# A list scheduler's estimated lengths are replaced by other ones, and its model of the port and of transposes is rewritten

## Chip, cores and metric

The kernel runs on one core of one Trainium2 chip. The metric is the device time of one execution in microseconds; the time of a kernel is the median of several executions. Before the change three executions gave 1193.82, 1195.94 and 1197.42 us.

## What is computed

A "macaron" block on x of shape 4 x 2048 x 256 in float32: half a feed-forward, one causal attention head, half a feed-forward, each behind a layernorm and with a residual. All feed-forward products run on operands that are first rounded, in blocks of 16, to a 4-bit grid.

```python
x = x + 0.5 * ffn(layernorm(x), w_gate, w_up, w_down)
x = x + attn(layernorm(x), Wq, Wk, Wv)          # causal softmax, scale 1/16
x = x + 0.5 * ffn(layernorm(x), w_gate, w_up, w_down)

def fp4_linear(x, w):                            # both sides rounded per block of 16
    return einsum('bsk,nk->bsn', fp4(x), fp4(w))
def fp4(x):
    scale = max(max(abs(block)) / 6, 1e-12)
    return nearest_on_grid(block / scale) * scale   # 0 .5 1 1.5 2 3 4 6, signed
def ffn(x, w_gate, w_up, w_down):                # 256 -> 704 -> 256
    return fp4_linear(silu(fp4_linear(x, w_gate)) * fp4_linear(x, w_up), w_down)
```

## The kernel before

**Tiling.** The 8192 rows are cut into 32 "pairs" of 2 x 128 rows (8 pairs for each of the 4 sequences). A pair n passes through these steps, each a small function of the kernel; the names are used below:

- `load(n)`, `ln_first(n)`: DMA of the rows (tile `xt`), first layernorm. Sums and squares are on ScalarE (ACT), a chain of seven two-element operations (`ve`, `rs`, `r2` ..., `nm`; tiles with prefix f, a or g for the three layernorms) on GpSimd (POOL), and the last scaling on ACT again (tile `xn`).
- `x1(n)`: the rounding of `xn` (tiles `xs`, `xinv`, `xf`, `xsh`, `xsl`) on VectorE (DVE) and ACT, and a DMA transpose to `xqT`.
- `gu1(n)`: 48 matmuls, for each half pair 12 into a gate tile `pg` and 12 into an up tile `pu`; ACT applies silu to `pg`, DVE multiplies with `pu` (tile `h`). `pg` and `pu` have one PSUM buffer each, so the next gate matmuls wait until ACT has read the last ones.
- `hh1(n)`: the rounding of `h` (tiles `hs`, `hinv`, `hf`, `hsh`, `hsl`) on DVE and ACT, two DMA transposes to `hT`.
- `down1(n)`: 2 x 17 matmuls on `hT` into `po`, and a DVE operation that adds them to `xt`.
- `lnattn(n)`, `xattn(n)`, `vy(n)`: second layernorm, two transposes to `xT`, the products for values (`vv`) and for the combined query/key matrix (`y`).
- `scores(n,j)`, `exps(n,j)`, `pv(n,j)` for each half pair j: scores into `ps`, copied out by DVE into `sc` with a running maximum (`mc`, `mr`, `nb`); exp on ACT; a split into two float16 halves (`pp`), one to three transposes to `pT`; the product with `vv` into `po`, scaled by `rc` and added to `xt`.
- `lnlast(n)`, `x2`, `gu2`, `hh2`, `down2(n)`: the third layernorm and the second feed-forward, and the store of the rows.

`prepare_gu`, `prepare_dn` and `prepare_attn` round, scale and transpose the weights at the start. The last pair (31) is finished in two half pairs, called z0 and z1 below; its steps are written out at the end of the kernel.

**Order.** All operations are first only recorded, in a software-pipelined order (pairs n+6 to n-3 in one step). Then `order` plans: a list scheduler (`_pass`) plays the five instruction queues PE, ACT, DVE, POOL and SP with an estimated length (`_cost`: time on the engine, `busy`, and time until a reader may use the result, `late`) for each operation, and emits them in the order of planned start. It is run forward and backward 6 times for each of 15 settings in `POLICIES` (how far ahead an operation may be taken, how strongly waiting counts, how far the first steps are pulled forward: `lead`), the setting that loses least planned PE time is kept for each half of the run, and one last pass writes the order. The order on each engine is then fixed: an instruction waits for its operands, and all that stands behind it in its queue waits too. All DMA is issued from SP's queue. Each instruction is emitted from one line (`emit`, line 362 of the profile), so groups are told apart by their tiles.

**What the plan knows of POOL and the transposes.** POOL shares a port to the on-chip memory with DVE. Before, a POOL operation is not planned while a DVE operation that takes the port (`op.locks`) runs; it is put off, and DVE operations that lock get a malus of `PORT` meanwhile. Transposes are planned as one queue (`served`) with 1.7 ns an element.

Of the kernel before, what the change touches and what calls it, by code (L numbers as in the profile page):

```python
# [12 lines left out]
F32 = mybir.dt.float32  # L13
# [4 lines left out]
AF = mybir.ActivationFunctionType  # L18
ALU = mybir.AluOpType
# [33 lines left out]
LN2 = 0.6931471805599453  # L53
BYTES = {F32: 4, I32: 4, F16: 2, BF16: 2, U16: 2}
SWITCH = 17600.0
PORT = 500.0
ROUNDS = 6
POLICIES = [(soon, 60.0, lead) for lead in (0.0, 10000.0, 20000.0) for soon in (50.0, 100.0, 150.0, 200.0, 300.0)]
MIDDLE = 500000.0
RATE = 330.0  # L60
LATENCY = 1900.0
WINDOW = 3413.0
IDLE = 0.42

# [90 lines left out]
class Record:  # L155
# [53 lines left out]
    def _cost(self, op):  # L209

        size = lambda v: v.at.size
        views = op.outs + op.ins
        n = max(map(size, views[:1] + (op.ins[:1] if op.method == "tensor_reduce" else [])))
        psum = any(v.tile.pool.psum for v in views)
        accum = isinstance(op.kwargs.get("accum_out"), View)
        if op.engine == "PE":
            t = max(n, 64) / 2.4 + 2.2
            if op.ins[0].dtype == F32:
                t *= 2 if op.method == "transpose" or "is_transpose" in op.kwargs else 4
            return t, t + 65  # L220
        if op.engine == "SP":
            if op.method == "dma_start_transpose":
                return 1240, 2250 + max(0, n - 500) * 1.2
            op.load = n * 4 * P / RATE if op.outs else 0
            return 490, LATENCY + op.load + 500 * (not op.outs)
        if op.engine == "POOL":
            t = 110 if op.method == "memset" else 850 if ALU.pow in op.args else 350
            return t, t
        if op.engine == "ACT":
            t = 95 + n * (0.75 if psum else 0.833) + 90 * accum  # L230
            t += 90 * sum(isinstance(op.kwargs.get(k), View) for k in ("scale", "bias"))
            return t, t + 105 * (not accum)
        many = sum(size(v) > 1 for v in op.ins)
        op.locks = not psum and (many > 1 or op.method == "tensor_scalar" and BYTES[op.ins[0].dtype] == 2)
        fast = not psum and all(BYTES[v.dtype] == 2 for v in views)
        if op.method == "reciprocal":
            t = 60 + 6.25 * n
        else:
            t = 65 + n * (1.042 if not fast else 0.26 if op.method == "tensor_scalar" else 0.52) + 65 * accum
        return t, t + 95  # L240

    def order(self):

        for pool in self.pools:
            for ring in pool.rings.values():
                for k, t in enumerate(ring):
                    if k >= t.n:
                        t.first.deps.update(dict.fromkeys(ring[k - t.n].ops, True))  # L250
                    if k:
                        t.first.deps.setdefault(ring[k - 1].first, False)
                    t.first.deps.pop(t.first, None)
        for op in self.ops:
            for u in op.after:
                op.deps.setdefault(u, False)
            op.users = {}
        for op in self.ops:
            for u, data in op.deps.items():
                u.users[op] = u.late + 24 if data else u.busy  # L260

        best = [None, None]
        for policy in POLICIES:
            lead = {op: op.lead * policy[2] for op in self.ops}
            rank = {op: 88.0 * op.index - lead[op] for op in self.ops}
            for _ in range(ROUNDS):
                start, out, end = self._pass(rank, False, policy, policy)
                for h, value in enumerate(self._lost(start, end)):
                    if best[h] is None or value < best[h][0]:
                        best[h] = (value, policy, start, rank)  # L270

                back, _, _ = self._pass({op: -start[op] - op.busy for op in self.ops}, True, policy, policy)
                rank = {op: -back[op] - op.busy - lead[op] for op in self.ops}
        (_, one, start, rank1), (_, two, _, rank2) = best

        part = {op: min(1.0, max(0.0, (start[op] - MIDDLE) / 50000.0 + 0.5)) for op in self.ops}
        rank = {op: rank1[op] * (1.0 - part[op]) + rank2[op] * part[op] for op in self.ops}
        return self._pass(rank, False, one, two)[1]
# [7 lines left out]
    def _pass(self, rank, back, one, two):  # L286


        free = dict.fromkeys(("PE", "ACT", "DVE", "POOL", "SP"), 0.0)
        waiting, held = {e: [] for e in free}, ("PE", "POOL")  # L290
        ready, start = dict.fromkeys(self.ops, 0.0), {}
        if back:
            nxt, left = {op: [] for op in self.ops}, {op: len(op.users) for op in self.ops}
            for op in self.ops:
                for v, lag in op.users.items():
                    nxt[v].append((op, v.busy + lag - op.busy))
        else:
            nxt, left = {op: list(op.users.items()) for op in self.ops}, {op: len(op.deps) for op in self.ops}
        for op in self.ops:
            if not left[op]:  # L300
                waiting[op.engine].append(op)
        kept = False
        table, out, end, landed, served, locked, clock = None, [], 0.0, 0.0, 0.0, 0.0, Counter()
        while len(out) < len(self.ops):
            best = None
            if not any(waiting.values()):
                raise RuntimeError("the order goes in a circle")
            for e, ops in waiting.items():
                if ops:
                    t = max(free[e], min(ready[op] for op in ops))  # L310
                    if best is None or t < best[0]:
                        best = (t, e)
            t, e = best
            soon, patience = (one if t < MIDDLE else two)[:2]
            now = [op for op in waiting[e] if ready[op] <= t + soon]
            op = min(now, key=lambda o: (
                rank[o] + patience * max(0.0, ready[o] - t) + SWITCH * (o.table is not None and o.table != table)
                + PORT * (kept and e == "DVE" and o.locks)
            ))
            t = max(t, ready[op])  # L320
            if e == "POOL" and not back and op.method != "memset":

                kept = t < locked
                if kept:
                    free[e] = locked + 1.0
                    continue
            if op.table is not None and op.table != table:
                table, t = op.table, t + 1290
            waiting[e].remove(op)
            out.append(op)  # L330
            start[op], more = t, 0.0
            if back:
                pass
            elif e == "PE":

                k = int(t // WINDOW)
                more = op.busy if k and clock[k - 1] < IDLE * WINDOW else 0.0
                clock[k] += op.busy + more
            elif op.load:
                landed = max(landed, t + LATENCY) + op.load  # L340
                more = landed - t - op.late
            elif e == "SP" and op.outs:
                served = max(served + 1.7 * op.outs[0].at.size + 100, t + op.late)
                more = served - t - op.late
            elif e == "DVE" and op.locks:
                locked = t + op.busy
            elif e == "POOL" and op.method != "memset":
                more = (775.0 if ALU.pow in op.args else 275.0) - op.busy
            free[e] = t + op.busy + (more if e in held else 0.0)
            end = max(end, t + op.late + more)  # L350
            for u, lag in nxt[op]:

                ready[u] = max(ready[u], t + lag + (more if e in held or u.deps.get(op) else 0.0))
                left[u] -= 1
                if not left[u]:
                    waiting[u.engine].append(u)
        return start, out, end
# [787 lines left out]
```

## Time and profile before

| | before |
|---|---|
| median of three runs | 1195.94 us (1193.82 to 1197.42) |
| the profiled execution's own time | 1194.8 us |
| span of that execution on the core | 1193.1 us |
| PE busy | 1156.1 us, 97% |
| DVE busy | 1064.1 us, 89% |
| ACT busy (84 table loads of 1283 ns among it) | 845.4 us, 71% |
| POOL busy | 254.9 us, 21% |
| DMA transposes | 411 issues of four kinds, median 2.5 to 3.8 us to landing |

Busy times are those of the profiled execution; they are unions of the instructions' spans, and a matmul's end is modelled, so a busy PE may still lose a little between matmuls. The time outside the span is 1.7 us. Each text line of the profile's groups has engine, operation, result and operands by tile name, and how often.

### The profile page before, as it was taken

To read this page: it belongs to the slowest core of one execution; us is meant where nothing else is said; L and a number is where in the kernel's file an instruction comes from. 1 tells how busy PE (TensorE), PEld (TensorE's weight loads), DVE (VectorE), ACT (ScalarE), POOL (GpSimd) and SP (SyncE) were. 2 spreads that over 40 slices of the span, in tenths; PEclk is the share of its full clock that TensorE was granted. 3 is DMA by queue.
4 is the path that set the end of the run, shared out by engine and by line. 5 is a ranking of instruction groups with operands and counts; after the bars stand their busy time and mean duration, and the time that the engine had idled before them with its cause. 6 is when DMAs were issued, how large, how long until landed. Compare 5 with 4: busy or idle time off the path is not lost.

```text
span 1193.1 us, 23867 instructions
## 1 busy us (share of the span) xinstructions
PE 1156.1 (97%) x8665; PEld 843.8 (71%) x8665; DVE 1064.1 (89%) x2677; ACT 845.4 (71%) x1694; POOL 254.9 (21%) x706
## 2 busy tenths in 40 slices
PE   3999999999999999999999999999999999999997
PEld 1676677777687777777777777777777777777775
DVE  8998999998879999998888999999887999978776
ACT  8788886676568777775776986776758776766552
POOL 4122331121032222212222230222212222010020
PEclk9999999999999999999999999999999999999999
DMA  7353646763665565655755465666556454665553
GB/s 236 55 100 71 109 88 110 140 129 71 107 131 103 105 116 120 113 93 111 134 102 81 95 114 104 131 131 120 92 104 113 88 93 87 114 117 96 102 111 85
DMA packets 452710, 128.92 MB, mean 108 GB/s; under 512 B 434672, under 2 KB 451824, under 8 KB 452592
## 3 DMA queue, kind: packets, MB, share of 16 engines
q1 hardware_dynamic: 452592, 127.39, 57.0%
q8 instruction: 68, 1.11, 0.4%
q14 instruction: 50, 0.41, 0.1%
HBM read 11.34 MB, written 8.39 MB: 17 GB/s over the span
## 4 chain that ended last, share of the span: by engine, by line
PE 68%; DVE 15%; ACT 12%; issue 2%; DMA 2%; POOL 1%; SPq 0%; DVEq 0%; ACTq 0%
PE po L362 30%; PE pg L362 14%; PE pu L362 14%; PE ps L362 10%; DVE h L362 5%; ACT xn L362 3%; ACT L362 2%; DVE hs L362 2%; ACT hf L362 2%; ACT h L362 1%; DVE xt L362 1%; DMA hT<-h 1%; ACT pp L362 1%; DVE xs L362 1%; DVE sc L362 1%
## 5 line engine op out<-in xcount | busy, mean ns | idle before, releaser
L362 PEld LDWEIGHTS <-xqT 128*128 128x128 f16 x3072 | 299.7, 98 | 161.1 <-issue 6.2
L362 PE MATMUL po<-wdT,hT 128*128 128x256 f16 x2176 | 262.6, 274 | 5.9 <-DMA hT<-h 5.6
L362 PE MATMUL pg<-wguT,xqT 128*128 128x384 f16 (+1 forms) x1536 | 258.9, 312 | 4.3 <-ACT h L362 2.3
L362 PE MATMUL pu<-wguT,xqT 128*128 128x384 f16 (+1 forms) x1536 | 253.3, 312 | 0.1
L362 PEld LDWEIGHTS <-hT 128*128 128x128 f16 x2176 | 213.2, 98 | 39.8 <-DMA hT<-h 7.6
L362 PE MATMUL ps<-xT,y 128*128 128x512 f16 (+2 forms) x960 | 200.9, 347 | 1.0 <-DVE mc L362 1.0
L362 PE MATMUL po<-vv,pT 128*128 128x257 f16 (+1 forms) x1632 | 194.4, 272 | 0.4
L362 PEld LDWEIGHTS <-pT 128*128 128x128 f16 x1632 | 157.9, 97 | 33.3 <-issue 2.3
L362 ACT ACTIVATE h<-pg,cgu 128x704 f32<-128x704 f32 x128 | 108.1, 845 | 93.9 <-PE pg L362 91.2
L362 DVE TENSOR_TENSOR h<-h,pu 128x704 f32<-128x704 f32 x128 | 113.2, 884 | 50.9 <-PE pu L362 33.4
L362 PEld LDWEIGHTS <-y 128*128 128x128 f16 x960 | 90.9, 98 | 69.6 <-ACT y L362 1.2
L362 ACT ACTIVATE hf<-h 128x1408 f16<-128x1408 bf16 (+1 forms) x65 | 88.1, 1355 | 65.1 <-DVE h L362 65.0
L362 ACT ACTIVATE sc<-sc,nb,ksc 128x128 f32<-128x128 f32 (+7 forms) x64 | 82.7, 1292 | 38.6 <-DVE nb L362 38.0
L362 ACT ACT_TABLE_LOAD x84 | 107.8, 1283 | 2.1 <-PEq L1138 0.8
L362 DVE TENSOR_REDUCE hs<-h 128x88 f32<-128x1408 f32 (+1 forms) x65 | 103.7, 1595 | 1.0
L362 DVE TENSOR_TENSOR h<-h,hinv 128x1408 f32<-128x1408 f32 (+1 forms) x65 | 103.8, 1597 | 0.4
L362 DVE TENSOR_SCALAR_CACHE_REDUCE sc<-ps 128x512 f32<-128x512 f32 (+2 forms) x144 | 84.7, 595 | 11.5 <-PE ps L362 11.2
L362 DVE TENSOR_TENSOR pp<-sc,pp 128x1024 f16<-128x1024 f32 (+4 forms) x96 | 86.1, 907 | 5.7 <-ACT pp L362 5.0
L362 POOL TENSOR_SCALAR gve<-gsq 128x2 f32<-128x2 f32 (+1 forms) x33 | 9.4, 284 | 380.3 <-ACT xn L362 380.2
L362 POOL TENSOR_SCALAR ave<-asq 128x2 f32<-128x2 f32 x32 | 14.1, 439 | 327.4 <-ACT xn L362 277.7
L362 ACT CAST pp<-sc 128x1024 f16<-128x1024 f32 (+4 forms) x96 | 73.1, 789 | 1.0
L362 DVE SCALAR_TENSOR_TENSOR xt<-po,het,xt 128x256 f32<-128x256 f32 x128 | 59.5, 464 | 11.7 <-PE po L362 11.6
(153 smaller groups left out, 1593.6 us busy)
## 6 DMA issues: line engine op xcount, KB each, us to landing
xt<-x SPq DMA_DIRECT2D x32, 256.0 KB, 3.3
out<-xt SPq DMA_DIRECT2D x31, 256.0 KB, 2.6
pT<-pp SPq DMA_TRANSPOSE x152, 3.0
hT<-h SPq DMA_TRANSPOSE x128, 3.8
gu<-wgu SPq DMA_DIRECT2D x3, 384.0 KB, 5.0
xqT<-xn SPq DMA_TRANSPOSE x65, 3.2
xT<-xs SPq DMA_TRANSPOSE x64, 2.5
dwork<-wdn SPq DMA_DIRECT2D x1, 704.0 KB, 7.3
```

Source lines behind the costliest of these rows:

```text
L362: op.call(*map(real, op.args), **{k: real(v) for k, v in op.kwargs.items()})
```

## The change

Only the plan's model is edited; no operation of the computation is added, removed or altered. The lengths in `_cost` change (TensorE's results are taken as readable 176 ns instead of 65 ns after the matmul, POOL operations as 154 and 647 ns instead of 350 and 850, transposes as longer by their size, accumulating DVE operations as shorter, those with a per-row scalar as longer). The lag between an operation and its reader depends on the two engines (`_lag`). The malus `PORT` and the putting off of POOL operations are gone: a POOL operation that starts while DVE holds the port is planned as ending 35 ns before DVE does, and it is taken only when ready. A table load begins when ACT's queue is free. Instructions are themselves fetched by DMA; the plan now counts the instructions of PE, DVE and ACT, foresees when the next block is fetched (`FETCH`), and takes a transpose that meets such a fetch as late by 0.7 or 1.5 us; SP's queue is held when transposes back up.

```diff
-PORT = 500.0
+FETCH = {
+    "PE": (2.0, 256.0, 118.0, 64.0, 1500.0),
+    "DVE": (1.16, 128.0, 55.0, 470.0, 700.0),
+    "ACT": (1.26, 128.0, 60.0, 700.0, 700.0),
+}
...
-            return t, t + 65
+            return t, t + 176
...
-                return 1240, 2250 + max(0, n - 500) * 1.2
+                return 1280 + 0.13 * n + 0.75 * max(0, n - 1408), 1850 + 1.26 * n
...
-            return 490, LATENCY + op.load + 500 * (not op.outs)
+            return 570, LATENCY + op.load + 500 * (not op.outs)
...
-            t = 110 if op.method == "memset" else 850 if ALU.pow in op.args else 350
-            return t, t
+            t = 110 if op.method == "memset" else 647 if ALU.pow in op.args else 154
+            return t, t + 28
...
-            return t, t + 105 * (not accum)
+            t += 33 * (AF.Silu in op.args)
+            return t, t + 105
...
-            t = 65 + n * (1.042 if not fast else 0.26 if op.method == "tensor_scalar" else 0.52) + 65 * accum
+            t = 65 + n * (1.042 if not fast else 0.26 if op.method == "tensor_scalar" else 0.52) + 10 * accum
+            t += 62 * (op.method in ("tensor_scalar", "scalar_tensor_tensor") and any(size(v) == 1 for v in op.ins[1:]))
...
+    def _lag(self, u, op):
+        if op.engine == "POOL":
+            return 94 if u.engine == "POOL" else 101
+        return 81 if u.engine == "PE" and op.method == "tensor_tensor" else 48 if u.engine == "ACT" and op.engine == "PE" else 24
...
-                u.users[op] = u.late + 24 if data else u.busy
+                u.users[op] = u.late + self._lag(u, op) if data else u.busy
...
+            if e == "POOL":
+                soon = 0.0
...
-                + PORT * (kept and e == "DVE" and o.locks)
...
-            if e == "POOL" and not back and op.method != "memset":
-                kept = t < locked
-                if kept:
-                    free[e] = locked + 1.0
-                    continue
...
-                table, t = op.table, t + 1290
+                table, t = op.table, max(t, free[e] + 1400)
...
+            if e in FETCH:
+                i = list(FETCH).index(e)
+                per, block = FETCH[e][:2]
+                issued[i] += per - (e == "PE" and op.ins[0].dtype == F32)
+                if issued[i] > coming[i]:
+                    fetched[i], coming[i] = t, coming[i] + block
...
-                served = max(served + 1.7 * op.outs[0].at.size + 100, t + op.late)
-                more = served - t - op.late
+                begin = max(served, t + 1400)
+                served = begin + 1.26 * op.outs[0].at.size
+                held_up = 0.0
+                for i, (_, _, _, each, lost) in enumerate(FETCH.values()):
+                    for f in (fetched[i], t + max(0.0, coming[i] - issued[i]) * each):
+                        if begin - lost < f < served + 50:
+                            held_up = max(held_up, lost - max(0.0, begin - f))
+                served += held_up
+                more = served + 450 - t - op.late
+                free[e] = max(t + op.busy, served - 1850)
...
-                more = (775.0 if ALU.pow in op.args else 275.0) - op.busy
+                more = max([0.0] + [hi - t - 35.0 for lo, hi in locked if lo <= t < hi])
```

More of the change, by code (lines that the diff above doesn't have):

```diff
@@ L61 @@
 LATENCY = 1900.0
+WINDOW = 3413.0
+IDLE = 0.42
+FETCH = {
[3 more added lines that the diff above has]
+}
 WINDOW = 3413.0
@@ L301, in _pass @@
                 waiting[op.engine].append(op)
-        kept = False
-        table, out, end, landed, served, locked, clock = None, [], 0.0, 0.0, 0.0, 0.0, Counter()
+        fetched, issued = [-1e9] * 3, [0.0] * 3
+        coming = [first for _, _, first, _, _ in FETCH.values()]
+        table, out, end, landed, served, locked, clock = None, [], 0.0, 0.0, 0.0, [(0.0, 0.0)] * 2, Counter()
         while len(out) < len(self.ops):
@@ L342, in _pass @@
             elif e == "SP" and op.outs:
-                served = max(served + 1.7 * op.outs[0].at.size + 100, t + op.late)
-                more = served - t - op.late
+                begin = max(served, t + 1400)
[8 more added lines that the diff above has]
+                free[e] = max(t + op.busy, served - 1850)
             elif e == "DVE" and op.locks:
-                locked = t + op.busy
+                locked = [locked[1], (t, t + op.busy)]
             elif e == "POOL" and op.method != "memset":
-                more = (775.0 if ALU.pow in op.args else 275.0) - op.busy
-            free[e] = t + op.busy + (more if e in held else 0.0)
+                more = max([0.0] + [hi - t - 35.0 for lo, hi in locked if lo <= t < hi])
+            free[e] = max(free[e], t + op.busy + (more if e in held else 0.0))
             end = max(end, t + op.late + more)
```

## The prediction

> **What bounds the kernel now.** First the page's engine lines.
>
> ```profile
> span 1193.1 us, 23867 instructions
> ...
> PE 1156.1 (97%) x8665; PEld 843.8 (71%) x8665; DVE 1064.1 (89%) x2677; ACT 845.4 (71%) x1694; POOL 254.9 (21%) x706
> ```
>
> PE is busy all but 37.0 us (1193.1 - 1156.1). Its work stays, instruction for instruction, so an order can only win back part of those 37.0 us, or lose more. Where they lie, the table by stretches says (columns: length, then each engine's busy time and count, the granted clock, DMA).
>
> ```profile
> 0.00:40.00 40.00, 17.79 (x103) 11.77 (x104) 34.18 (x88) 34.27 (x94) 15.35 (x50) 1.00 0.61 183
> 40.00:80.00 40.00, 39.84 (x300) 29.10 (x298) 38.67 (x89) 26.37 (x52) 5.33 (x15) 1.00 0.50 88
> 80.00:160.00 80.00, 75.77 (x565) 54.28 (x563) 73.62 (x199) 70.72 (x162) 24.18 (x70) 1.00 0.47 85
> 160.00:200.00 40.00, 39.84 (x298) 28.60 (x296) 38.48 (x99) 27.73 (x58) 10.68 (x28) 1.00 0.71 126
> 200.00:1140.00 940.00, 938.41 (x7068) 686.43 (x7066) 839.78 (x2105) 665.45 (x1294) 194.97 (x529) 1.00 0.59 108
> 1140.00:1160.00 20.00, 20.00 (x169) 16.14 (x167) 16.00 (x36) 10.66 (x18) 3.81 (x12) 1.00 0.45 84
> 1160.00:1194.00 34.00, 24.43 (x176) 17.47 (x174) 23.39 (x65) 10.18 (x22) 0.56 (x3) 0.95 0.44 93
> ```
>
> PE's idle time is 22.2 us in the first 40, 4.6 from 40 to 200, **1.6 in the 940 us that follow**, and 8.7 from 1160 to the end (33.1 - 24.4). So three places count: head, a middle with nothing to win, and tail. The table of waits has, for PE from 200 to 700, one row, and in the tail this one above all (columns: total, times, longest):
>
> ```profile
> PE po L362 <- DMA hT<-h: 4.6, 2, 3.8
> ```
>
> Last the timeline of the tail, for the chain that the end hangs on.
>
> ```profile
> 1157.73 0.71 POOL L362 TENSOR_TENSOR gnm<-gnm,grs 128x1 f32<-128x1 f32 x1
> ...
> 1158.46 1.28 ACT L362 ACT_TABLE_LOAD   x1
> ...
> 1159.75 0.85 ACT L362 ACTIVATE h<-pg,cgu 128x704 f32<-128x704 f32 x1
> ...
> 1160.53 0.19 POOL L362 TENSOR_TENSOR gnm<-gnm,grs 128x1 f32<-128x1 f32 x1
> ...
> 1164.72 4.27 SPq L362 DMA_TRANSPOSE xqT<-xn  x2
> ...
> 1167.20 1.96 PE L362 MATMUL pg<-wguT,xqT 128*128 128x384 f16 x12 [0.19 <-DMA xqT<-xn]
> ...
> 1179.40 7.41 PE L362 MATMUL po<-wdT,hT 128*128 128x256 f16 x51 [3.77 <-DMA hT<-h]
> ...
> 1184.11 1.40 SPq L362 DMA_TRANSPOSE hT<-h  x1
> ...
> 1187.67 2.03 PE L362 MATMUL po<-wdT,hT 128*128 128x256 f16 x17 [0.86 <-DMA hT<-h]
> ```
>
> Half z0's normalised rows wait on POOL, then behind ACT's silu of pair 30; its transpose is issued at 1164.72 and read 2.48 us later. The last transpose takes 3.56 us to its first matmul, and 2.03 us of matmuls end the run.
>
> **What moves.** I set the orders of the two built kernels side by side. Of 8660 PE operations 7089 keep one common order, of 2212 on DVE 1231, of 1354 on ACT 855, of 702 on POOL 618, of 484 on SP 393. So it is a reshuffle of some microseconds everywhere. Table switches rise from 83 to 85: at 1.28 us a load that is 2.6 us on ACT, which is idle 29% of the span. In the middle PE hides them. Without that cover they cost 1.3 us each.
>
> The Trainium skill (ScalarE: Activation LUTs, What ACT_TABLE_LOAD costs) has 1.28 us for the load and 1.38 us of drain, 2.66 a switch, 5.3 us by it. The rows above show no drain after the load: it ends at 1159.74 and the silu starts at 1159.75.
>
> The malus that kept DVE off the port during POOL's operations is gone. The price is in two rows above: `gnm` takes 0.71 us in one half and 0.19 in the other, so one met lock costs about 0.5, at most one DVE operation of 1.6 (`h<-h,hinv` has a mean of 1597 ns). Seven operations make a chain. In the middle nothing on PE's path waits for it (1.6 us of idle in all). In the tail z0's and z1's chains are on the path: 0 to 1.6 us each. I take 0 in the sum, since the new order there has DVE in other operations; the range keeps the rest.
>
> **Middle, 200 to 1140: -0.5 (from -1.6 to +3).** For each matmul that reads or overwrites what another engine made I took the margin (its start minus the end of what it waits for), and for the new order the same with both read off this trace's clock at their new place in their engine's queue. Dependencies with under 2 us of margin, from 150 to 1140 us, go from 268 to 175. This is coarse, but says the middle does not get tighter. Little can be won: 1.6 us. The +3 is six new stalls of 0.5 us, the size of those that PE has from 80 to 160.
>
> **Head, 0 to 160: +0.5 (from -3.5 to +3).** DVE is 85 to 97% busy here, so places on DVE are times. The planner now settles on no pull for the first steps (`lead` 0 in place of 10000 ns). The 1.8 us reduction over w_down moves ahead of the scaling of the gate weights; the first matmul groups then start 1 to 2 us later. These wait in any case for ACT's silu of pair 0, whose place on ACT goes from 25.1 to 26.1 us of work: 1 us later. Against it, pair 1's `xqT` is ready 2.6 us of DVE work earlier and pair 3's 4.2. In the trace PE waits 0.63 us for pair 1's at 36.8 us and is full from there. So 36.8 stays within 1 us. From 80 to 160 PE idles 4.2 us, of it 3.3 in five waits of 0.3 to 1.0 us between 95 and 130. By the margins above, the consumers there are 1.0 to 1.2 us worse (`vy` of pair 2, `scores` of pair 2) and at 121 us 2.5 worse (`pv` of pair 1); others are better. All waits gone gives -3.5, all worse +3. I take +0.5, near no change.
>
> **Tail: +1.5 (from -2.4 to +4).** After `pv(31,0)` PE has 30.6 us of matmuls left in both orders; in the trace it takes 38.5 (1151.2 to 1189.7). The new order puts 19 of the 48 matmuls of `gu2(30)` before `pv(31,1)`, and 27 of `down2(29)` between the gate/up matmuls of z0 and of z1. `exps(31,0)` comes after `lnlast(30)`.
> 1. z0's rows are ready at 1153.5 as before. Its squares, 0.7 us, and POOL's chain, 2.6 to 3.1 us, end at 1157.7. ACT has no silu in the way, since `pg` of pair 30 ended at 1153.1: the normalising starts at 1157.9 in place of 1160.5.
> 2. On DVE come 1.2 us for z0, then 0.9 that wait for `pv(31,1)` (ends 1154.1 + 48 x 0.109 = 1159.3), the product of pair 30 (0.9) and the last 0.65: transpose at 1162.2, first matmul 2.48 later, 1164.7. That is 2.5 us earlier than 1167.2.
> 3. z0's 24 matmuls (3.6) and 27 of `down2` (2.95) keep PE to 1171.3. z1 has its rows at 1160.7, its normalised rows at 1164.6; DVE still has for pair 30 the block maxima, the reciprocals, and `h<-h,hinv` (1.6) in front. That makes its transpose 1171.8 and its first matmul 1174.3, where before it ran at 1170.8: **PE idles 3.0 us** where it had none.
> 4. z1's matmuls end at 1177.9. `hT` of pair 30 is issued 0.4 us later than before (1176.05 for 1175.66) and read at 1179.75.
> 5. On DVE z1's last rounding now stands behind an addition that needs `down2(30)`, half done at 1181.7. Then 0.35 + 0.1 + 0.8 for reciprocal and product, 0.75 on ACT, an addition (to 1184.15), 1.3 of DVE: the last transpose is issued at 1185.6 in place of 1184.11. So +1.5.
> Best case: the 2.5 us of step 2 reach the end. Worst: both POOL chains meet a lock on top, or the clock falls (below).
>
> The sum: -0.5 + 0.5 + 1.5 = +1.5, on the profiled 1194.8 us: 1196.3. That execution lies 1.1 below the median of 1195.94, so I expect **1197.4** as a median. A measurement here can tell about 0.3%, 3.6 us, from no change; the forecast is a change within it, chance 0.38.
>
> **Rival 1, slower: the clock falls in the new gap.** The trace shows it:
>
> ```profile
> 1176.71:1180.12 3.41, 0.72 (x7) 0.66 (x8) 3.41 (x12) 1.36 (x4) 0.00 (x0) 1.00 1.07 199
> 1180.12:1183.53 3.41, 3.41 (x19) 2.40 (x18) 2.73 (x11) 1.44 (x4) 0.00 (x0) 0.55 0.76 166
> ```
>
> After a stretch of 3.41 us in which PE worked 0.72, the granted clock fell to 0.55 for the next. The 51 matmuls there took 7.41 us, where 51 x 0.109 are 5.56. The gap of 3.0 us in step 3 may do the same earlier, before z1's 24 matmuls, at 1.7 us, straight on the path. With the head's +3 and the tail's +1.5 this is +6, 1202. It decides if one stretch has about 2.7 us of idle; the gap reaches that only if it falls mostly into one. Chance of slower by this or by stalls in the middle: 0.35.
>
> The Trainium skill (TensorE: Matmul & The Clock Gate, What's actually happening) lets the clock fall after a whole idle window of 3.4 us. By that a 3.0 us gap is free. The row differs: 0.72 us of work in the window did not save it.
>
> **Rival 2, faster.** The head's waits go (-3.5) and z0's 2.5 us reach the end: -6, 1190 as a median. For it: truer lengths put producers earlier where PE waits, and the margins in the middle grow. Against: the head's late consumers, and step 5. Chance 0.27.
>
> **Range.** The forecast alone is 1193.8 to 1201 (sum -3.6 to +3.6). Reaching to the rivals' values, 1190 and 1202, with a little for the measurement, 1189.5 to 1203.5 leaves out about 2 in 10.
>
> **What would show it.** PE idle from 200 to 1140 of 1 to 3 us; z0's first gate matmuls at 2.5 us earlier against the end of `pv(31,0)`; a gap of about 3 us before z1's gate matmuls; the last transpose about 34.4 us after that end (before 32.9); 86 table loads. I am wrong if PE's idle time falls under 30 us, or if the middle shows more than 5.

## The result, and the profile after

The changed kernel takes **1197.36 us** (median of 20 runs, 1195.64 to 1198.80), the kernel before, beside it, 1195.93 (20 runs, 1193.16 to 1197.48). The ratio is 1.0012, 95% interval 1.0006 to 1.0018: slower by 1.4 us, which is inside the 0.3% that was called no change. The forecast was 1197.4.

The profiled execution of the changed kernel took 1198.8 us, which is the top of its 20; that of before took 1194.8. The two traces therefore differ by 4.0 us where the medians differ by 1.4, and the sums below are of the traces. First the engine lines:

```profile
span 1197.1 us, 23878 instructions
...
PE 1156.4 (97%) x8665; PEld 845.8 (71%) x8665; DVE 1057.1 (88%) x2677; ACT 848.5 (71%) x1696; POOL 241.0 (20%) x706
```

The same 8665 matmuls; PE's idle time goes from 37.0 to 40.7 us (1197.1 - 1156.4). POOL and DVE are both less busy (by 13.9 and 7.0 us), and the time gains nothing by it. The stretches show where the idle time is:

```profile
0.00:40.00 40.00, 16.08 (x81) 9.95 (x82) 31.51 (x86) 30.92 (x88) 17.17 (x48) 1.00 0.64 182
40.00:80.00 40.00, 39.81 (x298) 29.25 (x297) 38.89 (x85) 26.16 (x54) 6.54 (x17) 1.00 0.45 82
80.00:160.00 80.00, 76.81 (x570) 55.60 (x568) 74.48 (x201) 68.81 (x157) 23.45 (x70) 0.98 0.47 84
160.00:200.00 40.00, 40.00 (x304) 29.25 (x302) 38.61 (x104) 31.06 (x65) 8.60 (x28) 1.00 0.73 133
200.00:1140.00 940.00, 937.32 (x7077) 687.25 (x7075) 834.39 (x2104) 669.41 (x1297) 180.72 (x529) 1.00 0.59 107
1140.00:1160.00 20.00, 20.00 (x168) 16.17 (x167) 15.93 (x37) 12.53 (x17) 2.66 (x7) 1.00 0.73 143
1160.00:1198.00 38.00, 26.38 (x181) 18.31 (x179) 23.29 (x66) 9.64 (x22) 1.81 (x7) 0.89 0.37 78
```

Against before: the head +1.7 (23.9 for 22.2), 40 to 200 us -1.2 (3.4 for 4.6), the middle +1.1 (2.7 for 1.6), the tail +2.0 (37.1 - 26.4 = 10.7 for 8.7), and in the tail the mean clock is 0.89 for 0.95. Two waits make most of the tail's idle time (total, times, longest):

```profile
PE po L396 <- DMA hT<-h: 4.2, 1, 4.2
PE pg L396 <- DMA xqT<-xn: 2.8, 2, 2.0
```

The second row is new in size. It is the gap ahead of z1's gate matmuls, as the timeline of the tail shows:

```profile
1151.83 1.95 PE L396 MATMUL pg<-wguT,xqT 128*128 128x384 f16 x12
1158.25 0.60 ACT L396 ACTIVATE xn<-xt,gnm,grs 128x256 f32<-128x256 f32 x1 [0.60 <-POOL gnm L396]
1162.76 10.64 SPq L396 DMA_TRANSPOSE xqT<-xn  x2
1166.01 1.96 PE L396 MATMUL pg<-wguT,xqT 128*128 128x384 f16 x12 [0.79 <-DMA xqT<-xn]
1174.70 2.77 PE L396 MATMUL pg<-wguT,xqT 128*128 128x384 f16 x12 [1.99 <-DMA xqT<-xn]
1177.27 2.86 PE L396 MATMUL pu<-wguT,xqT 128*128 128x384 f16 x12
1179.97 5.82 PE L396 MATMUL po<-wdT,hT 128*128 128x256 f16 x51
1182.35 0.48 DVE L396 SCALAR_TENSOR_TENSOR xt<-po,het,xt 128x256 f32<-128x256 f32 x1
1186.42 1.39 SPq L396 DMA_TRANSPOSE hT<-h  x1
1189.98 3.37 PE L396 MATMUL po<-wdT,hT 128*128 128x256 f16 x17 [4.19 <-DMA hT<-h]
```

`pv(31,0)` ends at 1151.8, 0.6 us later than before; from there to the last matmul's end (1193.35) are 41.5 us where before had 38.5; what follows is 0.4 longer. 0.6 + 3.0 + 0.4 are the 4.0 us. So in this execution the whole middle and head together give 0.6, and the tail 3.0. Of these 3.0, 1.7 pass until the last transpose is issued (34.6 us behind that end for 32.9), nothing more until its first matmul (3.56 us in both), and 1.34 in the last 17 matmuls. The durations tell what kind of loss it is: z1's 24 matmuls take 2.77 and 2.86 us where z0's take 1.95 each, and the last 17 take 3.37 where before took 2.03. The clock in those stretches (the last column but two):

```profile
1172.70:1174.70 2.00, 0.01 (x1) 0.00 (x0) 2.00 (x7) 0.19 (x1) 0.00 (x0) 1.00 0.33 66
1174.70:1176.10 1.40, 1.40 (x8) 0.88 (x9) 1.40 (x4) 0.00 (x0) 0.00 (x0) 0.86 0.00 0
1176.10:1179.50 3.40, 3.40 (x15) 1.74 (x13) 2.91 (x11) 2.06 (x5) 0.00 (x0) 0.56 0.79 149
1189.40:1192.90 3.50, 2.92 (x15) 2.06 (x16) 0.00 (x0) 0.00 (x0) 0.00 (x0) 0.52 0.09 31
```

The clock falls 1.0 us after the gap of 2.0 us is over, while PE already works (a mean of 0.86 over 1.4 us is 1.0 us at full and 0.4 at half), and stays at half for 3.4 us. It falls a second time at 1189.35, in the gap of 4.2 us, for 3.4 us again: that takes in nearly all of the last 17 matmuls. In the 20 runs the mean clock of the execution sorts the times: at 0.997 or more (9 runs) the mean is 1196.66, at 0.996 or less (11 runs) 1197.81. That alone proves nothing of the change, since the executions of before sort likewise (90 beside the experiments: 1195.2 as the mean of 35 at 0.999 or more, 1197.0 of 36 at 0.997 or less).

### The profile page after: what moved, and what is told of

Read it like the earlier page. It is cut to its first block, busy times and chain, and to the rows that moved or that the text cites. A ratio compares the mean times of both kernels' runs of the same rounds, so it can differ in the third digit from the quotient of the medians.

```text
span 1197.1 us, 23878 instructions
## 1 busy us (share of the span) xinstructions
PE 1156.4 (97%) x8665; PEld 845.8 (71%) x8665; DVE 1057.1 (88%) x2677; ACT 848.5 (71%) x1696; POOL 241.0 (20%) x706
## 4 chain that ended last, share of the span: by engine, by line
PE 89%; DVE 4%; ACT 3%; POOL 2%; DMA 1%; issue 1%; SPq 0%; ACTq 0%; DVEq 0%
PE po L396 39%; PE pg L396 18%; PE pu L396 18%; PE ps L396 14%; DVE h L396 1%; ACT xn L396 1%; DMA xqT<-xn 1%; DVE hs L396 1%; POOL fr L396 0%; DMA gu<-wgu 0%; POOL frs L396 0%; ACT L396 0%; DVE xs L396 0%; POOL ars L396 0%; DMA hT<-h 0%
## 5 line engine op out<-in xcount | busy, mean ns | idle before, releaser
L396 PE MATMUL pg<-wguT,xqT 128*128 128x384 f16 (+1 forms) x1536 | 261.7, 315 | 3.4 <-DMA xqT<-xn 3.0
L396 PE MATMUL pu<-wguT,xqT 128*128 128x384 f16 (+1 forms) x1536 | 259.2, 313 | 0.0
L396 PEld LDWEIGHTS <-hT 128*128 128x128 f16 x2176 | 213.2, 98 | 38.5 <-DMA hT<-h 5.8
L396 PE MATMUL ps<-xT,y 128*128 128x512 f16 (+2 forms) x960 | 203.7, 347 | 1.1 <-DVE sc L396 0.9
```

The lines of the kernel that those rows point to most:

```text
L396: op.call(*map(real, op.args), **{k: real(v) for k, v in op.kwargs.items()})
```

## The experiments

The time between the start of `pv(31,0)`'s 45 matmuls and the last matmul's end is called the tail below; it is 43.5 us in the trace of before and 46.5 in that of after. Experiments on the order fix a list of all operations in place of the planner's:

```diff
-        rec.emit(rec.order())
+        rec.emit([rec.ops[i] for i in ORDER])
```

**Theory:** the tail's new order costs the time, by a gap ahead of z1 and a clock that falls in it; head and middle are about even. **Rivals:** the head's late gate matmuls, or new single stalls in the middle.

### 1. The two orders spliced: old tail, new tail, old head

`ORDER` is one kernel's order up to 1116 us (150 us for the third) and the other's behind.

*New order, tail of before.* 

> The new order until the products of pair 30 with its values (1116 us of the trace of before), then the old order to the end. Theory (the tail costs 2 to 3.6 us, head +1.3, middle -1.5, so the two nearly cancel): 1195.5 to 1196 us as a median, 0 to 0.5 below before and 1.5 to 2 below the changed kernel. Rival (the loss is made in head and middle, the tail is only where the last wait shows): it stays at 1197.4, 1.4 above before.

Measured: 1202.40 us (5 runs), ratio 1.0054 (1.0041 to 1.0067). Neither value. The place of the splice has a stall of its own, since both orders have other operations in flight there:

```profile
PE ps L728 <- DVE sc L728: 4.2, 1, 4.2
```

Its tail is 44.7 us, shorter than after's 46.5, but a time with such a stall at the seam settles nothing.

*Old order, tail of after.* 

> The old order until the same place, then the new order. Theory: the tail alone adds 2 to 3.6 us, so 1198 to 1199.5 us, slower than both kernels. Rival (loss in head and middle): within 0.5 us of before, 1196.

Measured: 1198.12 (11 runs), ratio 1.0016 (1.0007 to 1.0025), 1.6 over the before of that chip (1196.52). That is the theory's value: the new tail alone brings about as much as the whole change. Here z1's gap is as long as in after, but z1's matmuls run at full speed:

```profile
1174.82 1.96 PE L728 MATMUL pg<-wguT,xqT 128*128 128x384 f16 x12 [1.99 <-DMA xqT<-xn]
...
1189.41 3.17 PE L728 MATMUL po<-wdT,hT 128*128 128x256 f16 x17 [3.42 <-DMA hT<-h]
```

So the same gap takes the clock in one execution and leaves it in another; only the last 17 were slowed here, by 1.14 us against before's 2.03.

*Old head, then the new order.* 

> The old order for the first 150 us, the new order from there. Theory: PE's idle time and cold clock in the first 160 us cost the changed kernel 1 to 2 us net, which go: 1195.5 to 1196.5 us. Rival (the later start of the first matmuls is made up by 160 us, as the idle time of -1.0 from 80 to 160 says): 1197.0 to 1197.8, as the changed kernel.

Measured: 1198.26 (11 runs), ratio 1.0017 (1.0008 to 1.0026). Nothing gained over after. The first 40 us have 22.0 us of idle again, but from 80 to 160 PE then idles 4.3 us for after's 3.2, and 1.4 from 160 to 200, behind the seam: what the head saves is lost by 200 us.

### 2. Keep the clock up in the new tail

27 matmuls of 512 columns whose result nothing reads: 9 of them in `ORDER` ahead of z1's gate, 18 ahead of the last 17.

```diff
+        warm = ps_sc.tile([P, 512], F32, name="ps")
+        for _ in range(27):
+            T.matmul(warm, minus, wdT[:, 0, 0:4, :].rearrange("p c t -> p (c t)"), start=True, stop=True)
-        rec.emit(rec.order())
+        rec.emit([rec.ops[i] for i in ORDER])
```

> The changed kernel with 27 matmuls of 512 columns added that nothing reads, 9 in PE's gap ahead of the last half pair's gate matmuls and 18 in the gap ahead of the last 17 matmuls, so that PE isn't idle there. Theory (the clock falls in these gaps, up to 1.7 us for the first and 1.3 for the second): 1195 to 1196.3 us, 1 to 2.4 below the changed kernel, the granted clock of all runs at 0.998 or more, and a narrower spread. Rival (the chain is on DVE and the transposes, the clock hurts only matmuls that wait anyway): 1197 to 1198.5.

Measured: 1196.01 (11 runs, 1195.50 to 1196.73), ratio 0.9999 (0.9990 to 1.0008), clock at or above 0.998 in every run. This is the theory's value. Against after's 1.0012 it is about 1.5 us (0.0013 of 1196): the excess of the change, and the spread shrinks from 3.2 to 1.2 us. The two ratios' intervals just touch, but the two kernels above that have the new tail and ran beside this one, 1198.12 and 1198.26, lie 2.1 and 2.3 us higher. PE and DVE in its tail:

```profile
1174.16 1.96 PE L729 MATMUL pg<-wguT,xqT 128*128 128x384 f16 x12 [0.43 <-DMA xqT<-xn]
...
1188.97 2.02 PE L729 MATMUL po<-wdT,hT 128*128 128x256 f16 x17
```

```profile
1181.06 0.48 DVE L729 SCALAR_TENSOR_TENSOR xt<-po,het,xt 128x256 f32<-128x256 f32 x1 [0.32 <-PE po L729]
```

The tail is 44.7 us, 1.8 less than after's: the last 17 matmuls take 1.35 less, and the last transpose is issued 33.8 us behind the end of `pv(31,0)` instead of 34.6. The run fills both gaps at once, so it does not tell on the median what either is worth. The last row matters for step 5 of the prediction: with the clock up, the addition that stands ahead of z1's rounding does wait for `down2(30)`, by 0.32 us.

*The same in before:* 16 ahead of the last 68, 4 ahead of the last 17. 

> The kernel before with 20 matmuls added that nothing reads, 16 in PE's gap of 3.8 us ahead of the last 68 matmuls and 4 ahead of the last 17, so that the clock stays up. Theory: the half clock made an addition on DVE wait 0.65 us, so 0.5 to 1 us off: 1195 to 1195.6, and a narrower spread. Rival (the spread and the drop have nothing to do with the time): same as before within 0.3 us.

Measured: 1196.07 (11 runs), ratio 1.0001 (0.9992 to 1.0010). No gain, as the rival said, and a spread of 2.9 us as ever, at clocks all at or above 0.999. In before the clock's fall, which the prediction read off the trace (51 matmuls in 7.41 us), costs the median nothing that can be measured. In the trace of this run the addition on DVE that waited 0.65 us for those matmuls waits no more, and the last transpose is issued 32.4 instead of 32.9 us behind `pv(31,0)`; but its first matmul comes 4.7 instead of 3.6 us after the issue, so that this execution shows no gain either.

### 3. Head and middle mended

In the new head, three copies of gate weights stand behind a normalising on ACT that waits for POOL. One edit to ACT's list takes them ahead of pair 2's and pair 3's:

```diff
+copy wguT<-pg (prepare_gu)
 activation xn<-xt,fnm,frs (ln_first 2)
-copy wguT<-pg (prepare_gu)
...
+copy wguT<-pu (prepare_gu)
+copy dwork (prepare_dn)
+copy wguT<-pg (prepare_gu)
 activation xn<-xt,fnm (ln_first 3)
```

> The changed kernel with ACT's copies of the gate weights moved ahead of the normalising of pairs 2 and 3, which waits 3.2 us for POOL there; the rest of the order is kept. Theory (POOL, met by DVE's port lock, holds ACT, ACT holds PE's first matmuls and keeps its clock at half until 31.7 us): the first gate matmuls 2 to 3 us sooner, PE's idle time up to 40 us 1.5 to 2 us less, and 1 to 2 us off the median: about 1195.5 to 1196.5 where the changed kernel has 1197.4 to 1198. Rival (DVE bounds the head whatever PE does): the median stays within 0.5 us of the changed kernel's.

Measured: 1197.45 (12 runs), ratio 1.0015 (1.0006 to 1.0024), as after. The runs fall into two groups, six from 1195.64 to 1196.82 at a mean clock of 0.997 or more and six from 1198.09 to 1200.37 at 0.996 or less, so the median says little here; the trace is of the second group (1199.32). The first gate matmuls run 2.8 us sooner (26.77 for 29.61), then wait for the next copy, and the second half's gate is at the same 35.91 us:

```profile
26.77 0.80 PE L728 MATMUL pg<-wguT,xqT 128*128 128x384 f16 x2
28.98 1.44 PE L728 MATMUL pg<-wguT,xqT 128*128 128x384 f16 x4 [1.41 <-ACT wguT L728]
...
35.91 1.95 PE L728 MATMUL pg<-wguT,xqT 128*128 128x384 f16 x12
```

*Three operations behind the longest stalls of the middle taken earlier* (at 100, 401 and 797 us):

```diff
 VectorE:
+scalar_tensor_tensor vv (vy 2)
 tensor_tensor xn<-xf,xsh (x1 5)
...
+tensor_scalar sc<-ps (scores 21,1)
 tensor_tensor xn<-xn,xinv (x1 26)
 ScalarE:
+activation vv<-po (vy 11)
 activation xn<-xt,fnm,frs (ln_first 15)
```

> The changed kernel with three operations moved a few places: DVE's copy of vv of pair 2 (PE waits 2.2 us for it at 100 us), ACT's copy of vv of pair 11 (1.8 us at 402) and DVE's copy of scores of pair 21 (0.9 us at 797). Theory (between stalls PE is full, so a stall removed there is won whole): the two stalls at 402 and 797 give 2.5 us, the one at 100 up to 2.2 us and the clock that fell behind it; 1193 to 1195.5 us. Rival (PE only meets the next late producer): under 1 us won, 1196.5 to 1197.5.

Measured: 1197.52 (11 runs), ratio 1.0013 (1.0004 to 1.0021). The stalls named are gone and others stand in their place; PE from 80 to 160 us first, then from 200 to 1140:

```profile
PE po L728 <- DVE y L728: 1.8, 1, 1.8
...
PE pg L728 <- ACT h L728: 1.1, 2, 0.6
```

In after these were `vv` with 2.2, and `vv` with 1.8 and `sc` with 0.9. Idle time of the middle falls by 1.1 us (1.5 for 2.7) and the median does not follow.

*All of it together* (head, middle, 27 unread matmuls). 

> The changed kernel with the head's, the middle's and the tail's edits together (ACT's copies first, three operations moved, 27 unread matmuls in the gaps). Theory (the three places are far apart and PE is full between them, so they add): -1.4 (tail) -1.5 (head) -3.5 (middle) from 1197.4, 1190 to 1192.5 us, faster than both kernels. Rival (they don't add, head and middle being bound by DVE): 1195 to 1196.

Measured: 1196.27 (11 runs), ratio 1.0004 (0.9995 to 1.0012). No better than the unread matmuls alone. The gains that were expected of the three do not add up.

### 4. z1's rounding first

In after z1's eight steps lie between the steps of pair 30's rounding on DVE. This edit changes DVE's list alone:

```diff
+xs, xs, xinv, xn, xsl, xf, xn, xn          (z1, all eight)
 hs, hs, hinv, het, h, h, ...               (pair 30, and z0's product)
-xs ... xsl ... xf, xn, xn                  (z1, between them)
...
-xt (down2 30, first half)
 het, hinv, hpt, h, hsl                     (z1's middle activations)
+xt (down2 30, first half)
-xt (down2 30, second half)
 hf, h, h                                   (z1)
+xt (down2 30, second half)
```

> After's order with two edits in VectorE's list alone: the eight steps that round z1's block of the last tile go ahead of pair 30's rounding instead of between its steps, and the two additions of down2(30) go behind the last steps of z1's middle activations. In after z1's steps take 2.16 us of VectorE and 0.64 us of ScalarE but lie from 1165.74 to 1172.07. Theory (the gap ahead of z1's first gate matmul and the clock that falls in it are what the new tail costs): z1's transpose is issued near 1169 instead of 1172.2, the gap of 2.0 us shrinks under 0.7 us, the last transpose is issued 1.5 to 3 us earlier; but TensorE then waits over 4 us for hT of pair 30, which VectorE can't make earlier, so the last 68 matmuls may start at half clock (up to +1.9). Together 1195.0 to 1196.8. Rival (VectorE's whole work sets the end of the tail, not the order within it): 1197.0 to 1198.0, and the last transpose still within 0.5 us of after's 34.6 us behind pv(31,0)'s end.

> The kernel with z1's rounding ahead, and 25 matmuls of 512 columns whose results nothing reads: 16 ahead of the last 68, 9 ahead of the last 17, each placed where TensorE waits. Theory: with the clock kept up the last 68 matmuls run at full clock and the time is 1193.8 to 1195.5, below before by 0.5 us or more. Rival (VectorE's work sets the end): equal within 0.5 us to after with its own 27 unread matmuls, 1195.7 to 1196.5.

Measured: 1201.64 (6 runs), ratio 1.0042 (1.0030 to 1.0055), and 1199.40 (10 runs), ratio 1.0027 (1.0018 to 1.0035), with the unread matmuls. Both far above what either side expected. The gap ahead of z1 went, as the theory said; the rest did not follow. DVE, ACT, PE and the queue of the first of the two:

```profile
1167.42 0.19 DVE L728 SCALAR_TENSOR_TENSOR xsl<-xs,xsh 128x32 f16<-128x32 f32 x1 [1.76 <-ACT xsh L728]
...
1166.42 0.85 ACT L728 ACTIVATE h<-pg,cgu 128x704 f32<-128x704 f32 x1 [2.82 <-PE pg L728]
...
1171.12 1.96 PE L728 MATMUL pg<-wguT,xqT 128*128 128x384 f16 x12
...
1181.17 8.16 PE L728 MATMUL po<-wdT,hT 128*128 128x256 f16 x51 [5.61 <-DMA hT<-h]
...
1188.50 1.96 SPq L728 DMA_TRANSPOSE hT<-h  x1
```

z1's `xsh` stands on ACT behind z0's silu, and that waits for PE until 1166.42. So DVE, which has z1's steps in front, stands for 1.76 us with pair 30's block maxima behind it; in after those filled the time. Pair 30's `hT` comes later, PE waits 5.61 us for it instead of 1.99 for z1's, and the 51 matmuls behind that wait run at half clock for 8.16 us. The additions of `down2(30)`, now near the end of DVE's list, then wait for them (0.49 and 0.75 us) ahead of the last transpose's producers. The tail is 50.7 us, and 49.4 with the unread matmuls; these did not do all they were meant to, as the 51 matmuls still take 7.41 us there. The interleaving that looked like the fault was what kept DVE busy.

### 5. The two halves of the change, each alone

New lengths without the foresight, planned anew:

```diff
-                held_up = 0.0
-                for i, (_, _, _, each, lost) in enumerate(FETCH.values()):
...
-                served += held_up
```

> After's scheduler without the part that takes transposes that meet an instruction DMA as late; the lengths, lags, POOL's model and the transposes' base model stay, and the scheduler plans anew. It chooses the policies (300, 60, 0) and (100, 60, 10000) where after has (200, 60, 0) and (100, 60, 0), so both halves have another order. In its tail pv(31,1) is two matmul groups earlier than in after, z1's rounding is less mixed with pair 30's, and the additions of down2(30) come behind the last transpose's producers. Theory (the tail's shape, which the policy happens to give, decides, and the planner's parts move the middle by under 1 us): 1195.3 to 1197.0. Rival (the lateness of transposes is what keeps TensorE fed in the middle): stalls on transposes in the middle, 1198.5 to 1202.

Measured: 1197.61 (11 runs), ratio 1.0013 (1.0004 to 1.0022). Neither expected value holds. In the trace its tail is as short as before's, 43.5 us, with z1's gap at 0.5 us:

```profile
1172.48 1.96 PE L390 MATMUL pg<-wguT,xqT 128*128 128x384 f16 x12 [0.51 <-DMA xqT<-xn]
...
1188.38 2.03 PE L390 MATMUL po<-wdT,hT 128*128 128x256 f16 x17 [2.21 <-DMA hT<-h]
```

From 0 to 160 us there is a wait on transposes that after does not have (0.8 there):

```profile
PE po L390 <- DMA hT<-h: 6.1, 5, 2.1
```

But the trace is of the fastest of the 11 executions (1195.52, at full clock), 2.1 us under their median. So where the median loses is not shown, and a short tail did not make this kernel fast.

Before's scheduler with the foresight alone:

```diff
+            if e in FETCH:
...
+                begin = max(served, t + op.late - 1.7 * op.outs[0].at.size - 100)
                 served = max(served + 1.7 * op.outs[0].at.size + 100, t + op.late)
+                held_up = 0.0
+                for i, (_, _, _, each, lost) in enumerate(FETCH.values()):
...
+                served += held_up
```

> Before's scheduler with only the foreseen instruction DMAs and the lateness of the transposes that meet one; all lengths, lags and POOL's model as before. Its policies are (100, 60, 10000) and (100, 60, 20000). In its tail, as in after, z1's gate matmuls come with only 13 matmuls of down2(29) after z0's, and VectorE mixes z1's rounding with pair 30's. Theory (the tail's shape decides, not which part of the planner was changed): the gap ahead of z1's gate matmuls is there, 2 to 4 us, and the time 1196.5 to 1199. Rival (the foresight is the useful part and the new lengths cost the 1.4 us): 1193.5 to 1195.5, with fewer waits on DMAs in the middle than before.

Measured: 1197.26 (11 runs), ratio 1.0008 (0.9999 to 1.0016). The time is the theory's, the reason is not: in the trace, of the slowest of the 11 (1199.08), z1's gate matmuls have no gap, and the tail of 45.8 us holds four waits on `hT`, 7.3 us in all. Within the intervals both halves alone are as slow as the two together, each with another tail. Neither half gains, and no half can be called the one that costs.

## Why the prediction was right, step by step

**The sum.** Forecast +1.5, measured +1.4 on the medians. That the two agree to 0.1 us is luck: the parts below miss by more than that, in both directions, and the traces differ by 4.0. The parts that carry it:

**Middle, -0.5: off in sign, inside its range.** Idle time of 2.7 us, 1.1 more than before, against a forecast of 1 to 3. The margins from 150 to 1140 us grew, and small starts-late did get fewer, but two single stalls (1.8 and 0.9) took the rest.

**Head, +0.5: a sub-step failed.** "So 36.8 stays within 1 us" is wrong: pair 1's gate is at 39.81, 3.0 us later, and the first gate matmuls 5.3 later (29.61 for 24.30) instead of 1 to 2. The estimate counted DVE's work, and missed two things in the trace of after, first POOL's, then ACT's row:

```profile
21.60 1.92 POOL L396 TENSOR_SCALAR fr<-fr 128x2 f32<-128x2 f32 x1
...
24.70 1.09 ACT L396 ACTIVATE xn<-xt,fnm,frs 128x256 f32<-128x256 f32 x2 [3.17 <-POOL fnm L396]
25.70 0.78 ACT L396 CAST wguT<-pg 128x768 f16<-128x768 f32 x1
```

A POOL operation of 0.19 us took 1.92 while DVE ran three operations on 16-bit data in 1.88 us, ACT waited 3.17 us for the chain, and the weights' copies stood behind it in its queue. I had priced a lock for the tail's POOL chains only. The +0.5 still held, by luck, since the loss shrinks: +1.7 of idle to 40 us, then -1.2 to 200. Both old head and mended head gave no time back, so what is lost here seems to be mostly repaid by slack behind it.

**Tail, +1.5.** On the clock from `pv(31,0)`'s end (1151.24 before, 1151.8 after, so 0.6 is added to each forecast):
- Steps 1 and 2: normalising at 1158.5, transpose issued 1162.8, forecast; 1158.25 and 1162.76 measured. The first matmul came 3.25 instead of 2.48 us behind the issue, so z0's gain is 1.8 and not 2.5 us. The price of the transpose was taken from one row.
- Step 3: z1's transpose at 1172.4 forecast, 1172.21 measured. The gap is there, 2.0 instead of 3.0 us, since PE itself came to it 0.8 us later (0.7 of it from z0's late transpose) and z1's first matmul 0.2 earlier.
- Step 4: `hT(30)` issued 1176.65 forecast, 1175.86 measured; 0.8 early.
- Step 5: last transpose 1186.2 forecast, 1186.42 measured, 34.6 us behind `pv(31,0)` against the forecast 34.4. The wait that was to cause it is not in this trace, though: z1's matmuls at half clock brought z1's product late, and DVE met the addition at 1182.35 with no wait. With the clock kept up the addition does wait (0.32 us), and the last transpose is issued at 33.8. So the step's mechanism is real and worth about 1.0 us over before's 32.9, not 1.5.
- The end, "2.03 us of matmuls", was taken over from before without a word on the clock. This is the step that failed. By the prediction's own steps 4 and 5 the gap ahead of the last 17 matmuls would be 3.9 us (from 1179.75 + 5.56 to 1185.6 + 3.56) where before had 0.86; it was 4.19 us, the clock fell in it, and they took 3.37 us.

**Rival 1 was half of the truth.** It gave a fall of the clock in z1's gap +1.7 on top of the forecast, and about 2.7 us of idle in one stretch as its condition. The fall came at 2.0 us, in some of the executions; in the trace of after it delays the last transpose by about 0.75 us (34.59 for 33.84 with the clock kept up, z1's first matmul being at 22.87 in both). The larger part is the last gap, which the rival did not name: in all five traces of the new tail without unread matmuls (after, old order with the tail of after, old head, head mended, middle mended) the last 17 matmuls take 3.14 to 3.81 us, while z1's are slowed in only three of them. By the warm runs the two falls together cost the median about 1.5. The forecast needed them: without, the change is worth -0.1 to before (ratio 0.9999). The term of +1.5 was therefore put on the wrong cause: the later transposes seem to be made good elsewhere, and what remains on the median is the clock. **Rival 2** fell: nothing of the head's waits went, and z0's gain was spent ahead of z1's gap.

The page "TensorE: Matmul & The Clock Gate" of the Trainium skill (section What's actually happening) lets the clock fall after an idle window of 3.4 us and calls the window free-running. Here PE worked in 1.42 of the 3.41 us ahead of the fall, so a whole idle window was not needed. The window that starts at its own time agrees with the traces (last section). It also corrects the reading of before's rows in the prediction: in finer slices before's clock falls at 1180.43, and in the 3.41 us ahead of that PE worked 1.03 us, not 0.72, so 2.7 us of idle was not the condition.

**What stays open.** Differences under 1 us between plans can't be placed: each plan's profiled execution is one draw from a spread of about 3 us. That the late transposes of the new tail are repaid elsewhere is only the difference of two medians, not shown in a trace. No run fills one of the two gaps alone, and the new lengths alone, with a short tail in their one trace, are as slow as the whole change.

## What to carry to other kernels

Here, where the main engine is busy 97% of the span, another model of lengths bought nothing by itself: the planner drew another order, and head, middle and tail each traded one late producer for another. Read what an idle gap does to the clock before counting only its length, and try a few unread matmuls in it: in after they were worth about 1.5 us, in before nothing. Look at the last gap first: the matmuls behind it end the run. And before a "late" chain is moved to the front of an in-order queue, look at what each of its steps waits for on the other queues: z1's rounding, put first, stopped DVE for 1.8 us, and the kernel became about 4 us slower.

## What the runs showed of the hardware

- **POOL beside VectorE.** A two-element operation of 0.19 us took 1.92 through three of VectorE's operations. The Trainium skill ("SBUF — State Buffer", section SBUF: two separate sides) has the loser of the shared ports blocked for the whole instruction; the row agrees, and shows that it may be held over several in a row. It need not be: in the trace with the mended head the same operation, beside the same three, took 0.58 us.
- **The clock after a gap.** In fine slices of these traces the granted clock is 1.00 or 0.50. In after, from 40 us to the last matmul, it falls at 103.91, 1175.70 and 1189.35 us and comes back 3.41 us later each time. The last two falls are 13.65 us apart, 4 x 3.41, and the first lies 314 such steps ahead of the second: the falls stand on one grid. In the tail PE's work within one stretch of it decides, and not the gap's length. The stretches around z1's gap, which is 2.0 us in the first three rows:

| trace | stretch of the grid (us) | PE's work in it | clock in the next |
|---|---|---|---|
| after | 1172.29 to 1175.70 | 1.42 | 0.50 |
| old order, tail of after | 1173.06 to 1176.47 | 1.65 | 1.00 |
| middle mended | 1172.46 to 1175.87 | 1.83 | 1.00 |
| before (its gap of 3.77 us) | 1177.02 to 1180.43 | 1.03 | 0.50 |

  In after the gap lies whole in one stretch; in the next two it is cut by the grid. The border is not sharp by this measure: near 100 us the clock also fell behind 1.59 (after) and 1.67 us (middle mended).
- **Table loads.** 86 instead of 84, as counted, cost nothing that the rows show; 84 and 88 in the two half changes go with the same times.
